# Two attention layers on one core: pairwise maxima for every query block, key, value and row work in one place, and one partial sum kept apart

## The chip, the cores and the metric

The kernel runs on one core of a Trainium2 chip. A core has five engines that run side by side and meet through semaphores: TensorE (PE; its weight loads are shown as PEld), VectorE (DVE), ScalarE (ACT), GpSimd (POOL) and SyncE (SP), which here only issues transfers. The metric is the device time of one execution in microseconds (us). All matrix products are float32.

## The reference

The input x has shape (2, 256, 64, 64). Two layers follow each other; each adds its input to its result.

```python
# layer 0: attention with 8 heads of d = 32 over n = 4096 pixels
qkv = einsum('oc,bchw->bohw', w_qkv, x)              # q, k, v: (b, 8, 32, 4096)
attn = softmax(einsum('bhdi,bhdj->bhij', q, k) / sqrt(32), axis=-1)
out  = einsum('bhij,bhdj->bhdi', attn, v)
x    = einsum('oc,bchw->bohw', w_proj, out) + x
# layer 1: a non-local block; phi and g are pooled 2x2 to 1024 pixels
f = einsum('bnc,bcm->bnm', theta(x[:, :64]), maxpool2(phi(x[:, 64:])))
y = softmax(f, axis=-1) @ maxpool2(g(x))
x = batchnorm(conv1x1(y, W)) + x
```

Layer 0 has 2 x 8 x 4096 x 4096 scores. Its softmax subtracts the row maximum, so all scores are computed twice: once for the maxima, once for the exponentials.

## The kernel before

**Tiling.** The 8 heads go in two quads of four; a quad's four heads of 32 channels fill the 128 partitions. n = 0..3 counts the pairs of batch and quad. A *block* is (n, i): 512 queries (i = 0..7) of the four heads against all 4096 keys. `attend` walks through a block in 32 steps, called *slots* here: slot j takes 128 keys. The loops run over quads, blocks, slots. After the two quads of a batch come `project` (the projection and the residual, which reuses x) and `non_local` (layer 1).

**One slot.** For each of two pairs of heads, `score` (L435) adds a product to the scores in PSUM and ScalarE takes the Exp of both heads at once, 128x1024 (L570). Scores are not recomputed from nothing: PSUM keeps those of the slot before, and the product is with a *difference of keys* (tiles `kd`, `last_kd`, `mid_kd`, `turn_kd`), so that the sum becomes the scores of the next keys. For j = 0 `subtract` (L447) first writes the negative row maximum. `weigh` (L459) multiplies the exponentials of the slot before by v into a scratch tile w, and VectorE adds w to the block's numerator in SBUF (L469; a copy for j = 0, L467). GpSimd adds up the exponentials of heads 0 and 1 (L487); those of heads 2 and 3 are summed by accumulating transfers that GpSimd issues every second slot (L493). `normalize` finishes the block before during the present one: at j = 1 a transfer joins two half sums (L502), at j = 5 GpSimd makes `whole` (L506), at j = 8 TensorE forms the denominators (L514) and ScalarE copies them (L522); SP moves them to DRAM and back so that few elements go to VectorE's reciprocal (L536), and some slots later GpSimd multiplies the numerator by the result (L545).

**Maxima ahead.** The maxima of a block are computed while the block before is in its slots, four slots ahead: the generator `maxes` is advanced twice per slot, each time by two of the four heads. A head's maximum over two chunks of 512 keys can be had in two ways. `plain` (L291): one product per chunk and a VectorE reduction of each (L294). `pair` (L296): max(a, b) = a + relu(b - a); a product with the difference of the two key chunks, a Relu on ScalarE into `over` (L301), a product with the first chunk, and `joint` (L308), a VectorE instruction that adds `over` and reduces both at once; reading its result out is a second short one. `of_head` says which head goes which way: heads 0 and 1 always plain; heads 2 and 3 by pairs, but in a quad's first block (i = 0, n > 0) only for the first half of the keys, as the differences of the second half, `last_kd`, still serve the quad before. After the last step VectorE reduces `part` to `neg` (L376), GpSimd splits that into three bfloat16 terms (`negate`, L141 to L145), and `make_rows` lets TensorE turn them into rows (L150), which ScalarE copies (L158). `first_block` does the very first maxima, all heads by pairs: in each two steps all four heads get their Relu, then all four their joint.

**Makes.** `make` produces a chunk of q, k or v from a chunk of x in the one buffer of the pool `xs` (tag "x"; SP loads it, L88). `during` lists three makes per block, which are done at slots 11, 19 and 27. From k come the differences, all on GpSimd: `differences` (L228), `between` (L237), `rounds` (L240); `renew` places them at the end of a quad's last block and at the start of the next. `late_weights` puts the weights for `project` and `non_local` into the same x buffer after the batch's last make.

**Order.** Each engine runs its instructions in one order. A scheduler makes it: it takes the program's order as priority, and moves an instruction up where its data and buffers allow. `tc.issue_after(ins)` makes what is traced in its block follow ins on ins's engine, and adds no wait. PSUM has four scratch buffers of one bank (`scratch`: products of the maxima, w, makes, rows, denominators, in turn) and two buffers of two banks (`scores`).

## Time and profile before

| what | us |
|---|---|
| median of three runs | 3921.29 (3920.49 to 3923.82) |
| the profiled execution | 3922.07 |
| its span, first to last instruction | 3920.3 |
| batch 0: start, to the first weighing | 0 to 107 |
| a regular block of quads 0 to 2 | 101.9 |
| block (0, 7) | 106.6 |
| a block of quad 3, i = 1 | 99.0 |
| TensorE / VectorE / ScalarE / GpSimd busy | 3884.4 / 2938.6 / 2655.8 / 3050.4 |

Blocks are measured from one block's first weighing to the next one's, from the start times of L459. "Busy" counts a matmul from its start to its modelled end; matmuls overlap, and one that waits for a buffer after its predecessor started can be counted too, so a busy TensorE is not necessarily one that streams. In a line of the timeline the first number is the start in us, the second the duration, the number after x counts merged instructions, and brackets give the idle time before it and what ended it. In a line of groups or windows the busy time stands before the count.

### The profile page before, as it was taken

How to read it: one execution, taken by the hardware profiler on the slowest of the kernel's cores; microseconds unless marked ns; L12 is line 12 of the kernel's file. 1: busy time of each engine (PE TensorE's matmuls, PEld its weight loads, DVE VectorE, ACT ScalarE, POOL GpSimd, SP SyncE). 2: the span in 40 equal slices, each digit the busy share in tenths (PEclk: the TensorE clock that was granted, in tenths of full speed). 3: DMA queues.
4: the chain of work that ended last, by engine and by line, in shares of the span. 5: the costliest groups of instructions: out<-in, count | busy, mean ns of one | idle time of the engine just before them, and what ended most of it. 6: DMA issues, size and time to landing. Idle time of an engine off the chain costs nothing.

```text
span 3920.3 us, 69961 instructions
## 1 busy us (share of the span) xinstructions
PE 3884.4 (99%) x27452; PEld 1374.6 (35%) x27452; DVE 2938.6 (75%) x5483; ACT 2655.8 (68%) x3296; POOL 3050.4 (78%) x1926
## 2 busy tenths in 40 slices
PE   8999999999999999999999999999999999999998
PEld 4333333333333333343333333333433333332333
DVE  5788888888888888874458888888888888884444
ACT  4778777777777777751137777777677788787111
POOL 1788888889888888871448888888899999996043
PEclk9999999999999999999999999999999999999999
DMA  1688888887887888880018888888888888888100
GB/s 57 135 169 169 167 169 169 173 170 166 166 170 166 167 168 168 173 198 6 22 38 167 168 172 170 170 171 174 165 175 168 168 169 169 167 167 184 57 16 27
DMA packets 113931, 569.40 MB, mean 145 GB/s; under 512 B 20296, under 2 KB 22600, under 8 KB 52416
## 3 DMA queue, kind: packets, MB, share of 16 engines
q0 software_dynamic: 68832, 501.25, 63.7%
q1 hardware_dynamic: 44080, 62.88, 4.6%
q8 instruction: 215, 3.52, 0.3%
q14 instruction: 116, 0.95, 0.1%
q10 hardware_dynamic: 688, 0.79, 0.1%
HBM read 54.78 MB, written 8.88 MB: 16 GB/s over the span
## 4 chain that ended last, share of the span: by engine, by line
PE 53%; DVE 2%; DMA 1%; ACT 0%; issue 0%; POOL 0%; DVEq 0%; ACTq 0%; POOLq 0%
PE s L435 14%; PE w L459 13%; PE ps L282 11%; PE y L732 6%; PE g L657 1%; DVE r L746 1%; PE f L700 1%; PE proj L600 1%; PE f L766 1%; PE q L194 1%; PE den L514 1%; PE tp L641 0%; PE tp L637 0%; PE v L182 0%; PE k L194 0%; DMA p<-p 0%
## 5 line engine op out<-in xcount | busy, mean ns | idle before, releaser
L487 POOL TENSOR_TENSOR p<-p,p 128x1024 f32<-128x1024 f32 x945 | 2350.6, 2487 | 375.1 <-ACT p L570 365.2
L570 ACT ACTIVATE p<-s 128x1024 f32<-128x1024 f32 x2048 | 2085.7, 1023 | 594.8 <-PE ps L282 529.1
L282 PE MATMUL ps<-k,q 32*128 32x512 f32 x6232 | 2020.1, 625 | 5.4 <-DVE part L308 3.4
L294 DVE TENSOR_REDUCE part<-ps 128x1 f32<-128x512 f32 x2136 | 1369.8, 686 | 548.0 <-PE ps L282 547.9
L459 PE MATMUL w<-p,v 128*32 128x512 f32 x8192 | 1091.9, 605 | 0.6 <-ACT p L570 0.6
L435 PE MATMUL s<-q,mid_kd 32*128 32x512 f32 x3072 | 766.3, 614 | 0.0
L469 DVE TENSOR_TENSOR y<-y,w 128x512 f32<-128x512 f32 x992 | 678.9, 684 | 59.2 <-PE w L459 58.8
L308 DVE CUSTOM_DVE_ANT_0 ps<-ps,over 128x512 f32<-128x512 f32 x980 | 675.4, 692 | 26.3 <-PE ps L282 23.1
L282 PEld LDWEIGHTS ps<-k,q 32*128 32x128 f32 x6232 | 631.9, 183 | 43.9 <-DVE part L308 10.1
L301 ACT ACTIVATE over<-ps 128x512 f32<-128x512 f32 x916 | 542.4, 592 | 9.2 <-PE ps L282 5.2
L282 PE MATMUL ps<-kd,q 32*128 32x512 f32 x1056 | 520.0, 591 | 0.0
L435 PE MATMUL s<-q,kd 32*128 32x512 f32 x2048 | 512.4, 615 | 0.4 <-ACT p L570 0.3
L435 PE MATMUL s<-q,last_kd 32*128 32x512 f32 x2048 | 510.2, 614 | 1.2 <-ACT p L570 1.2
L459 PEld LDWEIGHTS w<-p,v 128*32 128x32 f32 x8192 | 161.1, 108 | 804.5 <-DVE part L294 774.3
L282 PE MATMUL ps<-last_kd,q 32*128 32x512 f32 x904 | 441.7, 591 | 0.0
L435 PEld LDWEIGHTS s<-q,mid_kd 32*128 32x128 f32 x3072 | 261.8, 183 | 412.7 <-ACT over L301 226.4
L493 POOL DMA_DIRECT2D p<-p x448 | 395.2, 882 | 4.5 <-issue 3.1
L435 PEld LDWEIGHTS s<-q,kd 32*128 32x128 f32 x2048 | 177.7, 183 | 295.7 <-ACT over L301 174.4
L435 PEld LDWEIGHTS s<-q,last_kd 32*128 32x128 f32 x2048 | 177.2, 183 | 276.8 <-ACT over L301 162.7
L732 PE MATMUL y<-p,kv 128*128 128x512 f32 x512 | 240.0, 608 | 6.4 <-DVE r L746 6.4
L781 ACT ACTIVATE p<-f 128x1024 f32<-128x1024 f32 x64 | 65.5, 1023 | 248.5 <-PE f L766 219.2
L728 POOL TENSOR_TENSOR sums<-sums,p 128x512 f32<-128x512 f32 x96 | 121.4, 1264 | 114.3 <-ACT p L781 110.5
(117 smaller groups left out, 2683.2 us busy)
## 6 DMA issues: line engine op xcount, KB each, us to landing
p<-p POOLq DMA_DIRECT2D x478, 1024.0 KB, 7.6
x_q<-in_x_dram SPq DMA_DIRECT2D x30, 512.0 KB
x_k<-in_x_dram SPq DMA_DIRECT2D x24, 512.0 KB
x_res<-in_x_dram SPq DMA_DIRECT2D x16, 512.0 KB
out_dram<-z SPq DMA_DIRECT2D x16, 512.0 KB
r<-flat SPq DMA_DIRECT2D x120, 64.0 KB
x<-in_x_dram SPq DMA_DIRECT2D x8, 512.0 KB
x_v<-in_x_dram SPq DMA_DIRECT2D x6, 512.0 KB
```

Source lines behind the costliest of these rows:

```text
L282: nc.tensor.matmul(ps, q[n, i][bass.ts(h, D), bass.ts(g, P)], keys[bass.ts(h, D), :], start=True, stop=True,)
L294: reduced = nc.vector.tensor_reduce(part[:, g, h, j : j + 1], ps, AX.X, ALU.max)
L301: cut = nc.scalar.activation(over, ps, AF.Relu)
L308: reduced = nc.vector.tensor_tensor_reduce(out=ps, in0=ps, in1=over, scale=1.0, scalar=LEAST, op0=ALU.add, op1=ALU.max, accum_out=part[:, ...
L435: nc.tensor.matmul(s[:, t, :], kj[bass.ts(h, D), :], q[blk.n, blk.i][bass.ts(h, D), :], start=False, stop=True, skip_group_check=j > 0,)
L459: nc.tensor.matmul(w[bass.ts(h, D), :], v[blk.n][:, keys(j), h, :], p[h // 2][:, h % 2, :], start=True, stop=True,)
L469: nc.vector.tensor_add(blk.num, blk.num, w)
L487: added = nc.gpsimd.tensor_add(blk.sums[0], blk.sums[0], p[0])
L493: sent = nc.gpsimd.dma_start(out=blk.sums[n], in_=two, accum_op=ALU.add)
L570: nc.scalar.activation(p[pair], s, AF.Exp, scale=scale)
L728: nc.gpsimd.tensor_add(acc[i][NC], acc[i][NC], p[:, j, :])
L732: nc.tensor.matmul(acc[i][o], wg[:, 2 * t + j, bass.ts(o, P)], p[:, j, :], **edge)
```

## The change

It has four parts.

1. *Maxima by pairs throughout.* `of_head` lets heads 2 and 3 go by pairs in every block. The second-half differences of a new quad are made by GpSimd at slot 8 of the last block of the quad before (`before_all`), into a tile `first_kd` in the x buffer; `pair` reads them there for i = 0. ScalarE copies them to `last_kd` at slots 0 and 2 of the new quad's first block. The first-half differences move from the k make to slots 12 and 14 of block 4. VectorE's reset of `part` goes.
2. *Key, value and rows in one gap.* `during` now gives slots: q at 11, k and v of the same chunk together at 30, where the rows are made too; the last two blocks of a quad differ as shown. The rows get one buffer instead of two.
3. *One sum apart.* In slot j = 26 ScalarE copies w to SBUF (`apart`) in place of VectorE's addition; GpSimd adds it to the numerator at slot 18 of the next block, four steps into what was a wait of 13 steps in `normalize`; the multiplication comes one slot earlier.
4. *First maxima shifted.* In `first_block` heads 2 and 3 run one slot behind heads 0 and 1, so that a slot has the Relus of two heads and the joints of the other two. There is one slot more, and one `advance(maxes)` more.

```diff
-            to = work.tile([P, NB], BF16, tag="rows", name=f"rows_{name}")
+            if layer == 0:
+                to = work.tile([P, NB], BF16, tag="rows", name=f"rows_{name}", bufs=1)
+            else:
+                to = work.tile([P, 2, NB], BF16, tag="over", name=f"rows_{name}")[:, 0, :]
...
-        elif what == "k" and i == NI // 2 - 1:
-            kd[n] = qkv.tile([P, NI // 4, NB], F32, tag="kd", name=f"kd_{n}")
-            for c in range(2):
-                differences(n, c, kd[n][:, c, :])
...
         elif (i, j) == (NI - 1, NJ - 2):
-            differences(n + 1, 2, last_kd[:, 0, :])
             between(n + 1, 2)
-        elif (i, j) == (0, 0):
-            differences(n, 3, last_kd[:, 1, :])
         elif (i, j) == (0, 2):
             rounds(n)
+        if i == 0 and j in (0, 2):
+            nc.scalar.copy(last_kd[:, j // 2, :], first_kd[n][:, j // 2, :])
+    first_kd = {}
     def during(n, i):
         if i < NI - 2:
-            return [("q", n, i + 2), ("k", n + 1, i), ("v", n + 1, i)]
+            return {11: [("q", n, i + 2)], NJ - 2: [("k", n + 1, i), ("v", n + 1, i)]}
         if i == NI - 2:
-            return [("k", n + 1, i), ("k", n + 1, i + 1), ("q", n + 1, 0)]
-        return [("v", n + 1, i - 1), ("v", n + 1, i), ("q", n + 1, 1)]
+            return {
+                11: [("k", n + 1, i), ("v", n + 1, i)],
+                19: [("q", n + 1, 0)],
+                NJ - 2: [("k", n + 1, i + 1), ("v", n + 1, i + 1)],
+            }
+        return {7: [("q", n + 1, 1)]}
+
+    def before_all(n):
+        held.clear()
+        first_kd[n] = xs.tile([P, NI // 4, NB], F32, tag="x", name=f"first_kd_{n}")
+        for c in range(2):
+            differences(n, NI // 4 + c, first_kd[n][:, c, :])
...
-        ps = product(n, i, g, h, (kd[n] if jp < NI // 4 else last_kd)[:, jp % (NI // 4), :])
+        those = kd[n] if jp < NI // 4 else first_kd[n] if i == 0 and n > 0 else last_kd
+        ps = product(n, i, g, h, those[:, jp % (NI // 4), :])
...
     def first_block():
...
+        order = [(jp, g) for jp in range(NI // 2) for g in range(NB // P)]
+        over = {}
+        for slot in range(2 * len(order) + 1):
+            todo = []
+            for two, at in ((0, slot), (2, slot - 1)):
+                if not 0 <= at < 2 * len(order):
+                    continue
+                jp, g = order[at // 2]
+                if two == 0 and at % 2 == 0:
+                    t = double(f"over_{jp}_{g}")
+                    over[at // 2] = t.rearrange("p a b n -> p (a b) n")
+                s = scores(f"ps_{jp}_{g}_{at % 2}") if two else None
+                if at % 2 == 0:
+                    keys = (kd[0] if jp < NI // 4 else last_kd)[:, jp % (NI // 4), :]
+                else:
+                    keys = k[0][:, bass.ts(2 * jp, NB)]
+                for h in (two, two + 1):
+                    ps = product(0, 0, g, h, keys, s[:, h - 2, :] if two else None)
+                    todo.append((ps, over[at // 2][:, h, :], g, h, jp, at % 2))
+            for ps, o, g, h, jp, second in todo:
+                if second:
+                    joint(ps, o, g, h, jp)
+                else:
+                    nc.scalar.activation(o, ps, AF.Relu)
+            yield
...
-        chunks = 0 if h < 2 else NI // 2 if i == 0 and n > 0 else NI
+        chunks = 0 if h < 2 else NI
...
-        if i == 0 and n > 0:
-            nc.vector.memset(part[:, :, 2:, :], LEAST)
...
             if j == 0:
                 nc.vector.tensor_copy(blk.num, w)
+            elif j == NJ - LEAD - 2 and (blk.n, blk.i) != (len(QUAD) - 1, NI - 1):
+                blk.apart = work.tile([P, NB], F32, tag="apart", name=f"w_{blk.name}", bufs=1)
+                nc.scalar.copy(blk.apart, w)
             else:
                 nc.vector.tensor_add(blk.num, blk.num, w)
...
-                for _ in range(13):
+                for _ in range(4):
+                    yield
+            if blk.apart is not None:
+                with tc.issue_after(added.ins):
+                    nc.gpsimd.tensor_add(blk.num, blk.num, blk.apart)
+            if (blk.qd, blk.i) != (QUADS - 1, NI - 1):
+                for _ in range(8):
                     yield
...
+                        if i == NI // 2 and j in (12, 14) and blk.n + 1 < len(QUAD):
...
+                            with tc.issue_after(added.ins):
+                                differences(blk.n + 1, j // 2 - 6, kd[blk.n + 1][:, j // 2 - 6, :])
+                        if (i, j) == (NI - 1, 8) and blk.n + 1 < len(QUAD):
+                            with tc.issue_after(added.ins):
+                                before_all(blk.n + 1)
-                    elif j % 8 == 3 and j > 8 and items:
-                        advance(make(*items.pop(0)), 9)
+                    for item in items.get(j, ()):
+                        if item[1] < len(QUAD):
+                            advance(make(*item), 9)
```

More of the change, by code (lines that the diff above doesn't have):

```diff
@@ L135, in conv_attention, with negate @@
     nc.gpsimd.memset(t, 0.0)
-    def negate(name, neg):
+    def negate(name, neg, layer=0):
         rest = work.tile([P, NB // P, QH], F32, tag="rest", name=f"rest_{name}")
@@ L319, in first_block @@
     def first_block():
-        for jp in range(NI // 2):
-            for g in range(G):
-                over = double(f"over_{jp}_{g}").rearrange("p a b n -> p (a b) n")
-                for what in range(2):
-                    if what == 0:
-                        keys = (kd[0] if jp < NI // 4 else last_kd)[:, jp % (NI // 4), :]
-                    else:
-                        keys = k[0][:, bass.ts(2 * jp, NB)]
-                    s = scores(f"ps_{jp}_{g}_{what}")
-                    ps = [
-                        product(0, 0, g, h, keys, s[:, h - 2, :] if h >= 2 else None)
-                        for h in range(QH)
-                    ]
-                    for h in range(QH):
-                        if what == 0:
-                            nc.scalar.activation(over[:, h, :], ps[h], AF.Relu)
-                        else:
-                            joint(ps[h], over[:, h, :], g, h, jp)
-                    yield
+        order = [(jp, g) for jp in range(NI // 2) for g in range(NB // P)]
[23 more added lines that the diff above has]
+            yield
     G = NB // P
     def of_head(n, i, h):
-        chunks = 0 if h < 2 else NI // 2 if i == 0 and n > 0 else NI
+        chunks = 0 if h < 2 else NI
         pairs = [(g, jp) for jp in range(chunks // 2) for g in range(G)]
@@ L416, in __init__ @@
                 self.last = []
+                self.apart = None
         def keys(j):
@@ L550, in attend @@
                 blk = Block(qd, i)
-                items = [x for x in during(blk.n, i) if x[1] < len(QUAD)]
+                items = during(blk.n, i)
                 both = [None, None]
@@ L583, in attend @@
                                 renew(i, j, blk.n)
-                    elif j % 8 == 3 and j > 8 and items:
-                        advance(make(*items.pop(0)), 9)
+                        if i == NI // 2 and j in (12, 14) and blk.n + 1 < len(QUAD):
+                            if j == 12:
+                                kd[blk.n + 1] = qkv.tile(
+                                    [P, NI // 4, NB], F32, tag="kd", name=f"kd_{blk.n + 1}"
+                                )
+                            with tc.issue_after(added.ins):
[6 more added lines that the diff above has]
+                            advance(make(*item), 9)
         weigh(*waiting)
@@ L710, in maxima1 @@
                 nc.vector.tensor_copy(neg[:, :, 2], neg[:, :, 0])
-                ready.append(negate(f"l1_{b}_{i}", neg))
+                ready.append(negate(f"l1_{b}_{i}", neg, 1))
                 yield
@@ L806, in conv_attention @@
         advance(maxes, G)
+    advance(maxes)
     advance(make("q", 0, 1), 3)
```

## Prediction

> **What bounds the kernel now.** I read the shares first, then the table of windows for whole blocks, then the timelines of TensorE (PE) and VectorE (DVE) at the places that the change touches.[...]
>
> ```profile
> PE 3884.4 (99%) x27452; PEld 1374.6 (35%) x27452; DVE 2938.6 (75%) x5483; ACT 2655.8 (68%) x3296; POOL 3050.4 (78%) x1926
> ```
>
> PE is busy all the way, but pipelined matmuls count as busy while they wait for a buffer, so the length of stages has to decide. Windows of the start, of block (0,7), of the regular block (1,1) and of block (3,2):
>
> ```profile
> core 0: us, PE busy (x) PEld busy (x) DVE busy (x) ACT busy (x) POOL busy (x), PEclk, DMA share, GB/s
> 15.80:80.90 65.10, 61.66 (x313) 26.81 (x312) 45.09 (x129) 37.72 (x72) 8.57 (x7) 1.00 0.01 4
> 820.20:926.80 106.60, 106.60 (x827) 42.26 (x826) 90.24 (x164) 73.69 (x86) 94.03 (x57) 1.00 0.76 159
> 1028.70:1130.70 102.00, 102.00 (x812) 35.07 (x808) 83.27 (x163) 80.03 (x101) 91.50 (x54) 1.00 0.81 168
> 3053.90:3152.80 98.90, 98.90 (x795) 32.98 (x792) 83.16 (x163) 79.01 (x99) 90.38 (x53) 1.00 0.82 169
> ```
>
> In regular blocks no other engine fills its window: a plain slot lasts 2.96 us (weighing starts at 570.00, and at 603.48 and 606.44 in the same timeline), and PE streams through it: six groups of four row-tiled matmuls at 0.43 us, 2.56, plus 0.4 at the two changes of tiling. So a regular block is shortened only by fewer switches. Block (0,7) does the same matmuls and takes 4.7 us more, with VectorE at 90. The start has both engines waiting. TensorE around a k make, a v make and a row transpose:
>
> ```profile
> 570.00 1.06 PE L459 MATMUL w<-p,v 128*32 128x512 f32 x8
> 571.00 1.98 PE L194 MATMUL k<-x_k,wqk_sb 128*128 128x512 f32 x4
> 572.91 0.70 PE L435 MATMUL s<-q,mid_kd 32*128 32x512 f32 x2
> ...
> 596.58 2.05 PE L182 MATMUL v<-wv_sb,x_k 128*128 128x128 f32 x16
> 598.56 0.70 PE L435 MATMUL s<-q,mid_kd 32*128 32x512 f32 x2
> ...
> 607.44 0.40 PE L150 MATMUL pt<-ident_b,terms 128*128 128x128 bf16 x4
> 607.76 0.70 PE L435 MATMUL s<-q,last_kd 32*128 32x512 f32 x2
> ```
>
> From a make's start to the next scores: k 1.91 us, of which four matmuls stream 4 x 0.43 = 1.71; v 1.98, of which 16 x 0.111 = 1.78. Each lone make pays about 0.20 for the switch; the transpose 0.32 for 0.24.
>
> **What the skill says.** TensorEngine Tiling (Array Packing), Key Properties: changing the tiling mode drains TensorE; the 0.20 above agrees. The same page, PSUM Bottleneck: use both ScalarE and VectorE to empty PSUM, which the new ScalarE copy does. GPSIMD Engine Reference, Key points: GpSimd cannot access PSUM and is about 2x slower elementwise; so the copy is needed, and its 128x512 add takes 1.27 us (L237) beside VectorE's 0.68 (L469), 1.9x. DMA: Bandwidth & Descriptors, Latency and other measured facts, puts the fixed cost of a transfer near 2 us; here an 8 KB write issued at 1052.02 lets its successor go at 1056.45, 4.4 us, and I use that.
>
> **Part a, first maxima.** VectorE around one period (a make and four steps, 8 joints):
>
> ```profile
> 31.25 0.70 DVE L308 CUSTOM_DVE_ANT_0 ps<-ps,over 128x512 f32<-128x512 f32 x1
> ...
> 34.17 0.70 DVE L308 CUSTOM_DVE_ANT_0 ps<-ps,over 128x512 f32<-128x512 f32 x1 [2.17 <-PE ps L282]
> ```
>
> The period is 8.11 us (k makes at 30.13 and 38.24); eight of them make the 65 us. VectorE idles 2.2 us in each, because four Relus must run before the first joint, and all four heads turn from Relu to joint together. Half-shifted heads give ScalarE two Relus and VectorE two joints in every slot. Floors of a period: VectorE 8 joints at the spacings that the same timeline has when nothing is missing (0.62, 0.65, 0.65, 0.91 per four) 5.66; PE 8 groups x 0.43 + 1.92 = 5.36; ScalarE 8 x 0.5 + 0.58 = 4.6. I take 6.2, half a microsecond over the highest floor for hand-overs: 8 x 1.9 = 15.3 saved. Ends: 5.7 (19.3) and 7.3 (6.5). The one extra step at the end runs beside the q make.
>
> **Part b, pairs throughout.** In block (0,7) VectorE reduces one by one for heads 2 and 3 too:
>
> ```profile
> 861.23 2.48 DVE L294 TENSOR_REDUCE part<-ps 128x1 f32<-128x512 f32 x4 [0.33 <-PE ps L282]
> ```
>
> Four reduces at 0.60 and the add 0.68 leave nothing over, so slots stretch to 3.4. With pairs a slot has 2 reduces and a joint, as elsewhere. Block (0,7) gives back 106.6 - 101.9 = 4.7 and (0,6), whose last slots already run it (102.5), 0.6; three quads: 16.0. ScalarE's 16 more Relus of 0.59 per quad fit as in regular blocks. The second-half differences move to j = 8 of block 7 (GpSimd, 2 x 1.4 us, needed at about slot 12); they wait for the q make of slot 7 to free the x buffer, and behind them stand the running sums, whose lag of one to three us the probability buffers take.
>
> **Part c, one gap.** k and v share a gap 24 times: 24 x 0.20; the rows join 21 of them: 21 x 0.08; 6.5 saved, ends 0 and 8. The same matmuls run, so nothing else changes. Each x load is issued on SP when the make before it has freed the buffer, at least 8 slots (24 us) ahead, as now; six fewer are issued.
>
> **Part d, weighted sums apart.** One maxima block ends at slot 27. In quads 0 to 2 a make there hides the surplus; in quad 3 nothing does (block (3,1), VectorE, then PE):
>
> ```profile
> 3033.87 1.89 DVE L294 TENSOR_REDUCE part<-ps 128x1 f32<-128x512 f32 x3 [0.39 <-PE ps L282]
> 3035.67 0.69 DVE L308 CUSTOM_DVE_ANT_0 ps<-ps,over 128x512 f32<-128x512 f32 x1
> ...
> 3036.53 0.29 DVE L376 TENSOR_REDUCE neg<-part 128x16 f32<-128x128 f32 x1
> 3036.73 0.68 DVE L469 TENSOR_TENSOR y<-y,w 128x512 f32<-128x512 f32 x1
> ```
>
> ```profile
> 3037.46 1.12 PE L282 MATMUL ps<-k,q 32*128 32x512 f32 x2
> 3038.51 1.07 PE L459 MATMUL w<-p,v 128*32 128x512 f32 x8
> ```
>
> The product at 3037.46 waits for the buffer of w, which the add frees at 3037.41; weighing to weighing is 3.90, 0.95 too long. This add (j = 26) is the one that becomes a copy. ScalarE has no Relu in that slot and stands idle from 3035.78 to 3036.78; w is complete about then, so a copy of 0.59 (L522's 586 ns) frees the buffer near 3036.4; behind it stands the Exp of 3036.78, which waits for scores until then anyhow. I leave 0.2 for the late reduces. Quad 3: 6 x 0.75 saved; quads 0 to 2, where the make leaves slot 27, pay 24 x 0.2 = 4.8. Net +0.3; the bad end is 24 x 0.95 = +23. GpSimd gets 1.27 us per block at slot 18, covered by its 8.5 idle us of 98.9; uncovered it would be 30 x 1.27 = 38.
>
> **Part e, costs.** The one x buffer holds the new differences until two ScalarE copies in the next quad's first block, which overwrite what block (1,7) reads to its last slot. The late weights use that buffer:
>
> ```profile
> 1729.48 0.39 SPq L103 DMA_DIRECT2D weights<-in_wproj_dram  x1
> ```
>
> They now start 14 us before the first projection (1743.9). Afterwards they can start only near 1743.5, behind slot 31 and a copy. Issue plus 4.4 and some transfer ends near 1749: +5.5, once, ends 3 and 8; the residual loads queue behind them on SP but meet an equally late projection. The six ScalarE copies at quad starts, 0.59 against about 0.3 idle per slot: +1 (0 to 3.5). GpSimd near slots 26 to 31 of block 7 loses the make's relief and has three differences, the product and the casts; the j = 31 transfer, the half sum and the denominators may slip, about +2 over three quads, less 0.7 for the 0.9 that block (3,0) loses there now: +1.3. One buffer for the rows costs nothing: written at slot 30, last read at slot 0.
>
> **Sum.** -15.3 - 16.0 - 6.5 + 0.3 + 5.5 + 1.0 + 1.3 = -29.7. The profiled execution took 3922.07 (span 3920.3), 0.8 above the median: 3892.4, less 0.8, 3891.6.
>
> **Rivals.** (1) The first maxima stay bound by their buffers (period 7.6 or more): for it speaks that the two score buffers and four scratch buffers are unchanged; against, VectorE's 2.2 idle us per period. 3891.6 + 11 = 3903, 3898 to 3912. (2) GpSimd becomes the bound: 90.4 of 98.9 busy now, 91.7 then, and about 98 of 98 in block 7. Against: its lag has two or three slots of probability buffers. Some 4 us in each of three transitions and a little per block: 3907. (3) The other side: the copy apart stands behind the next Exp in ScalarE's queue. That Exp waits for scores, the copy would end near 3038.4 and the product 1.0 later than now: 1.9 in each of 24 blocks, 1.0 in six, 52 in all: 3943. It decides from about 1.5 us a block. (4) The parts cancel: handover at its bad end and only half of parts a and c, near 3921.
>
> **How the numbers follow.** Forecast 0.64 (3874 to 3902), rival 1 0.14, rival 2 0.09, rival 3 0.09, rival 4 0.04. Rivals 1 and 2 are still faster by over 0.2% (7.8 us, about what a measurement here can tell): 0.87 faster, 0.04 same, 0.09 slower. The range 3872 to 3912 leaves out rivals 3 and 4 and a little of each tail.
>
> **What would show it.** a: 8 makes 6.2 apart before 66 us, VectorE's 2.17 waits gone. b: blocks (n,7) near 98 us (one make), all slots 2.96. c: pt, k and v in one run of about 3.95 us. d: slot 27 at 3.1 to 3.2 everywhere. e: TensorE waiting some 5 us for the weights after block (1,7). Wrong if slot 27 is 3.9 or more in quads 0 to 2, or if the makes at the start keep their 8 us.

## The result, and the profile after

The changed kernel takes 3907.98 us (median of six, 3904.02 to 3909.10) against 3920.89 before (median of six), a ratio of 0.9965 (0.9955 to 0.9975): 13 us faster, less than half of the 29.7 that were forecast. Its profiled execution took 3908.37, with a span of 3906.6; against the span before (3920.3) that is -13.7, and all sums below are made on these two spans.

The page's shares after the change:

```profile
PE 3864.0 (99%) x27452; PEld 1366.8 (35%) x27452; DVE 2900.7 (74%) x5449; ACT 2697.5 (69%) x3378; POOL 3091.5 (79%) x1957
```

TensorE runs the same 27452 matmuls. VectorE has 38 us less, ScalarE 42 and GpSimd 41 more: the work moved as the change says. The table of windows for the start (up to the q make), block (0,7), the first block of the next quad (1,0), the regular block (1,1) and block (3,2):

```profile
core 0: us, PE busy (x) PEld busy (x) DVE busy (x) ACT busy (x) POOL busy (x), PEclk, DMA share, GB/s
15.70:74.50 58.80, 58.25 (x312) 26.34 (x310) 43.45 (x123) 37.73 (x72) 8.56 (x7) 1.00 0.02 6
817.60:916.30 98.70, 98.70 (x791) 32.67 (x788) 82.82 (x162) 80.65 (x102) 94.42 (x57) 1.00 0.76 154
916.30:1020.40 104.10, 103.50 (x812) 35.89 (x808) 82.89 (x162) 80.48 (x102) 95.93 (x58) 1.00 0.84 179
1020.40:1122.20 101.80, 101.80 (x812) 35.41 (x808) 82.71 (x162) 80.75 (x102) 91.63 (x54) 1.00 0.81 169
3044.10:3142.30 98.20, 98.20 (x796) 32.75 (x794) 82.66 (x162) 79.62 (x100) 91.70 (x54) 1.00 0.82 170
```

Block (0,7) takes 98.7, near the 98 that were forecast, and VectorE is back at 83. Block (3,2) lost 0.8 us, where 0.75 were forecast. But (1,0), 101.9 before, now takes 104.1 with the same matmuls, GpSimd at 95.9 and the highest DMA share. From first weighing to first weighing:

| stretch | before | after | difference |
|---|---|---|---|
| start, to the first weighing | 107.3 | 102.9 | -4.5 |
| blocks 0 to 5 of quads 0 to 2, without (1,0) | 17 x 101.8 | 17 x 101.6 | -3.1 |
| blocks 6 and 7, each of quads 0 and 2 | 102.5 + 106.6 | 105.4 + 98.7 | 2 x -5.0 |
| blocks (1,6) and (1,7), without the wait for weights | | | -4.8 |
| (1,0) | 101.9 | 104.1 | +2.2 |
| (3,0) | 99.8 | 102.6 | +2.8 |
| blocks (3,1) to (3,5) | 5 x 98.95 | 5 x 98.1 | -4.1 |
| wait for the weights beyond the 1.0 us of before, then projection and layer 1 of batch 0 | 291.7 | 4.9 + 295.2 | +8.4 |
| (3,7), projection and layer 1 of batch 1 | 376.9 | 376.2 | -0.7 |

The blocks are nearly where they were forecast. The start, the change of batch (batch 0 to batch 1, between quads 1 and 2) and the first blocks of quads 1 and 3 are not. The -4.5 of the start holds +0.7 from ahead of the first period: the k make of chunk 2 begins at 14.75 here and at 14.01 before, but at 13.48 in the kernel with part 4 alone. From that make to the q make the stretch fell from 64.9 to 59.7, by 5.2. TensorE and VectorE around one make at the start:

```profile
28.57 1.98 PE L197 MATMUL k<-x,wqk_sb 128*128 128x512 f32 x4
30.49 0.70 PE L293 MATMUL ps<-kd,q 32*128 32x512 f32 x2
...
35.92 1.98 PE L197 MATMUL k<-x,wqk_sb 128*128 128x512 f32 x4
```

```profile
29.65 0.73 DVE L320 CUSTOM_DVE_ANT_0 ps<-ps,over 128x512 f32<-128x512 f32 x1
30.30 0.14 DVE L320 DVE_READ_ACCUMULATOR2_ANT part<- 128x1 f32 x1
31.85 0.70 DVE L320 CUSTOM_DVE_ANT_0 ps<-ps,over 128x512 f32<-128x512 f32 x1 [1.40 <-ACT k L211]
32.46 0.14 DVE L320 DVE_READ_ACCUMULATOR2_ANT part<- 128x1 f32 x1
32.75 0.70 DVE L320 CUSTOM_DVE_ANT_0 ps<-ps,over 128x512 f32<-128x512 f32 x1
```

The makes are 7.35 us apart, 8.11 before. VectorE runs eight joints without a hole and then waits 1.40 us (2.17 before): TensorE starts its make at 28.57, VectorE has used up its stock of products by 30.44, and the next products only begin at 30.49. The trace names ScalarE's copy of k as what ended the wait, but that copy starts at 30.60, after TensorE had gone on, and was done 0.7 us before the joint; it is merely the last semaphore to come.

The change of batch, TensorE before and after the projection's start:

```profile
1728.97 1.06 PE L476 MATMUL w<-p,v 128*32 128x512 f32 x8 [1.14 <-ACT p L598]
1734.85 16.30 PE L639 MATMUL proj<-y,weights 128*128 128x512 f32 x32 [4.81 <-DMA weights<-in_wproj_dram]
```

The wait is there, 4.81 us long, near the forecast 5.5. What was not forecast stands in the windows around it:

```profile
1726.00:1732.00 6.00, 2.89 (x24) 0.32 (x16) 3.28 (x6) 2.92 (x4) 5.92 (x5) 1.00 0.82 153
1732.00:1736.00 4.00, 1.15 (x2) 0.67 (x3) 0.00 (x0) 0.00 (x0) 4.00 (x4) 0.59 0.94 271
1736.00:1740.00 4.00, 4.00 (x7) 1.70 (x6) 0.00 (x0) 0.00 (x0) 1.55 (x2) 0.56 1.08 245
1740.00:1744.00 4.00, 4.00 (x10) 1.73 (x10) 1.22 (x1) 0.00 (x0) 0.00 (x0) 1.00 0.99 307
```

From 1732 to 1740 the granted clock (third number from the right) is 0.59 and 0.56, and the first five matmuls of the projection start 0.85 to 0.99 us apart instead of 0.43.

The start of (1,0): GpSimd before the change, where the block begins at 926.76, then GpSimd and ScalarE after it, where it begins at 916.31:

```profile
924.86 0.85 POOL L493 DMA_DIRECT2D p<-p  x1
...
932.50 0.87 POOL L502 DMA_DIRECT2D p<-p  x1 [0.85 <-DMA p<-p]
```

```profile
909.57 0.84 POOL L515 DMA_DIRECT2D p<-p  x1
...
915.22 1.27 POOL L236 TENSOR_TENSOR mid_kd<-k 128x512 f32<-128x512 f32 x1
916.42 0.85 POOL L515 DMA_DIRECT2D p<-p  x1
...
924.76 0.87 POOL L524 DMA_DIRECT2D p<-p  x1 [2.78 <-DMA p<-p]
```

```profile
931.69 1.02 ACT L598 ACTIVATE p<-s 128x1024 f32<-128x1024 f32 x1 [1.90 <-DMA p<-p]
939.28 1.02 ACT L598 ACTIVATE p<-s 128x1024 f32<-128x1024 f32 x1 [2.38 <-POOL whole L528]
```

The accumulating transfer of slot 31 (L515) goes out at 916.42, 0.1 after the end of block (0,7), where it went out 1.9 ahead of that end before; the transfer that joins the half sums (L524, called the half sum below) must wait for its landing; and two Exps wait for the probability buffers that these transfers hold.

### The profile page after: what moved, and what is told of

It reads as the page before. It is cut to its first block, busy times and chain, and to the rows that moved or that the text cites. A ratio compares the mean times of both kernels' runs of the same rounds, so it can differ in the third digit from the quotient of the medians.

```text
span 3906.6 us, 69965 instructions
## 1 busy us (share of the span) xinstructions
PE 3864.0 (99%) x27452; PEld 1366.8 (35%) x27452; DVE 2900.7 (74%) x5449; ACT 2697.5 (69%) x3378; POOL 3091.5 (79%) x1957
## 4 chain that ended last, share of the span: by engine, by line
PE 96%; DVE 2%; DMA 1%; POOL 1%; issue 0%; ACT 0%; DVEq 0%; POOLq 0%; ACTq 0%; SPq 0%
PE s L452 28%; PE w L476 26%; PE ps L293 23%; PE y L771 6%; PE q L197 2%; PE k L197 2%; PE v L185 2%; PE proj L639 1%; PE g L696 1%; DVE r L785 1%; PE f L739 1%; PE f L805 1%; PE den L536 1%; DMA p<-p 1%; PE tp L680 0%; PE tp L676 0%
## 5 line engine op out<-in xcount | busy, mean ns | idle before, releaser
L305 DVE TENSOR_REDUCE part<-ps 128x1 f32<-128x512 f32 x2046 | 1315.7, 686 | 566.8 <-PE ps L293 563.1
L320 DVE CUSTOM_DVE_ANT_0 ps<-ps,over 128x512 f32<-128x512 f32 x1025 | 706.2, 691 | 24.9 <-PE ps L293 10.5
L491 DVE TENSOR_TENSOR y<-y,w 128x512 f32<-128x512 f32 x961 | 659.1, 686 | 51.9 <-PE w L476 49.3
L313 ACT ACTIVATE over<-ps 128x512 f32<-128x512 f32 x961 | 569.3, 592 | 10.7 <-PE ps L293 7.9
L452 PEld LDWEIGHTS s<-q,mid_kd 32*128 32x128 f32 x3072 | 270.4, 183 | 443.5 <-ACT over L313 253.9
L515 POOL DMA_DIRECT2D p<-p x448 | 395.3, 882 | 27.3 <-ACT p L598 27.1
```

Of the source, the lines that this page charges most:

```text
L305: reduced = nc.vector.tensor_reduce(part[:, g, h, j : j + 1], ps, AX.X, ALU.max)
L313: cut = nc.scalar.activation(over, ps, AF.Relu)
L320: reduced = nc.vector.tensor_tensor_reduce(out=ps, in0=ps, in1=over, scale=1.0, scalar=LEAST, op0=ALU.add, op1=ALU.max, accum_out=part[:, ...
L452: nc.tensor.matmul(s[:, t, :], kj[bass.ts(h, D), :], q[blk.n, blk.i][bass.ts(h, D), :], start=False, stop=True, skip_group_check=j > 0,)
L491: nc.vector.tensor_add(blk.num, blk.num, w)
L515: sent = nc.gpsimd.dma_start(out=blk.sums[n], in_=two, accum_op=ALU.add)
```

## Experiments

Each ratio is to the kernel before, measured beside it; the changed kernel's own is 0.9965. An interval reaches about 0.1%, or 2 to 6 us, to each side, so the times alone do not settle differences of 3 or 4 us between two of the changed kernels; there the stretches in the traces carry the argument. Where nothing is said, the kernel computes everything.

### The start: is it the makes?

**Part 4 alone**, the new `first_block` in the kernel before:

```diff
 (kernel before)
-        for jp in range(NI // 2):
+        order = [(jp, g) for jp in range(NI // 2) for g in range(NB // P)]
 ...
+    advance(maxes)
     advance(make("q", 0, 1), 3)
```

> The kernel before with the shifted first maxima alone. Theory (ring of two slots): makes at the start 7.35 us apart instead of 8.11, one longer last period, so the first weighing near 103 us instead of 107.3 and about 3916.5 us. If the step of the prediction had held (6.2 us a period, 15 us) it would be 3906. All other parts are those of before, so nothing else may move.

Measured: 3915.85, ratio 0.9987 (0.9981 to 0.9994). The makes are 7.34 apart, the last stretch from make to q make 9.09, as in the changed kernel; all blocks stay as before. So part 4 is worth 5 us, where the 6.2 us periods would have made it 15, and what is missing at the start is missing in part 4 itself.

**The makes in two halves**, one step apart:

```diff
-        advance(make(what, 0, i), 3)
-        advance(maxes, G)
+        made = make(what, 0, i)
+        advance(made)
+        advance(maxes, 1)
+        advance(made, 2)
+        advance(maxes, G - 1)
```

> The changed kernel with each make among the first maxima cut in two: the half for the first 128 channels before the first step, the other half before the second. Same matmuls. Theory (VectorE starves because one make holds TensorE for 1.92 us and the buffers let it be only one to two slots ahead): the 1.40 us wait per period shrinks below 0.7, periods of 6.4 to 6.7, 3901 to 3903. Rival (the order on ScalarE, where the copy of k stands ahead of the next Relus, or the joints' own spacing sets the period): 7.3 as now, 3908.

Measured: 3905.00, ratio 0.9957 (0.9944 to 0.9969), not clearly apart from the changed kernel's; the period is 7.05, not 6.4 to 6.7. VectorE now waits twice:

```profile
30.45 0.70 DVE L320 CUSTOM_DVE_ANT_0 ps<-ps,over 128x512 f32<-128x512 f32 x1 [0.72 <-issue]
32.53 0.70 DVE L320 CUSTOM_DVE_ANT_0 ps<-ps,over 128x512 f32<-128x512 f32 x1 [0.42 <-PE ps L293]
```

0.72 + 0.42 is little less than 1.40. Either the length of a make is not the point, or something else comes in when a make lies open across a step: its buffer stays taken in the ring of four. The next kernel keeps the make in one piece and shortens it: it leaves out half of the channels in six k makes.

**Half a make**, in one piece:

```diff
-        for c in range(NC):
+        few_c = 1 if what == "k" and n == 0 and i >= 2 else NC
+        for c in range(few_c):
```

> The changed kernel in which the six k makes of chunks 2 to 7 among the first maxima multiply only the first half of the channels (two of the four TensorE stretches, 0.96 us instead of 1.92, are left out, so the first quad's keys are not those of the reference). The place of the make's buffer in the ring of four stays as it is. Theory 1, that the period of 7.35 us is set by how long one make keeps TensorE from VectorE's next products: VectorE's wait of 1.40 us in each period falls by about 0.96, the k periods fall to 6.4 us. Theory 2, that it is the ring, in which the make takes a place until ScalarE has copied it: the wait stays, periods 7.0 to 7.35, as halving the makes in two pieces gave (7.05).

Measured: 3906.66 in one execution; the k makes are 6.66 apart. TensorE's make and VectorE's wait:

```profile
32.41 1.12 PE L198 MATMUL k<-x,wqk_sb 128*128 128x512 f32 x2
39.07 1.12 PE L198 MATMUL k<-x,wqk_sb 128*128 128x512 f32 x2
```

```profile
34.99 0.70 DVE L321 CUSTOM_DVE_ANT_0 ps<-ps,over 128x512 f32<-128x512 f32 x1 [0.72 <-issue]
```

0.86 us less of make gives 0.68 less of waiting. So the wait follows the make's length, to four fifths. The shorter make also gives its buffer back earlier; but in the changed kernel TensorE goes on at 30.49, before the copy of k that frees this buffer has begun, so it is not that buffer that it waits for there. VectorE's stock of products hides a part of every make; a second half that follows a step later finds the stock not yet rebuilt, or its buffer missing (0.42 of waiting more), which is why two halves save only 0.3. Which of the two it is, no run tells apart.

### The pairs, and the weights that they delay

**Part 1 undone** in all quads, the rest kept:

```diff
-        chunks = 0 if h < 2 else NI
+        chunks = 0 if h < 2 else NI // 2 if i == 0 and n in (1, 2, 3) else NI
 ... (no before_all and no copies to last_kd; its differences at (NI - 1, NJ - 2) and (0, 0) as before)
```

> The changed kernel without its first part: in a quad's first block heads 2 and 3 go by single chunks for the second half of the keys again, and the second-half differences are made late, so the x buffer is never held. Theory (the pairs gain 5.0 us at each of three quads and lose 13 at the quads' starts and at the change of batch): about 3910, within 2 of the changed kernel. Rival (the loss lies elsewhere and the pairs are worth their 16 less some 7): 3917.

Measured: 3907.09, ratio 0.9962 (0.9949 to 0.9974): the same as with the pairs. Blocks (0,7) and (2,7) take 101.9 instead of 98.7, and (1,7) 3.0 more up to its last weighing, so the pairs are worth 9.4 us in three quads. In return the projection starts 0.99 us after the last weighing instead of 5.88, and projection and layer 1 take 291.4 instead of 295.2: 8.6 us at the change of batch. (3,0) takes 100.1 instead of 102.6, so 2.5 us of its stall go with the pairs. Gain and costs nearly cancel. (1,0) still takes 104.4: its stall does not come from the pairs.

**Undone for quad 2 alone**, so that the x buffer is free when batch 0 ends:

```diff
-        chunks = 0 if h < 2 else NI
+        chunks = 0 if h < 2 else NI // 2 if i == 0 and n in (2,) else NI
```

> The changed kernel with the first part undone for quad 2 alone, the one whose differences hold the x buffer across the change of batch. Theory (the late weights and the slow clock behind them cost 7 to 8 us there, the pairs bring 5): 3905, the projection of batch 0 starting within 2 us of the last weighing, its matmuls 0.43 us apart from the first. Rival (the weights cost no more than what the pairs bring, the loss is in the layer after): 3908 to 3913.

Measured: 3901.16, ratio 0.9947 (0.9934 to 0.9961), some 7 us better than the changed kernel, more than the 3 expected; the trace shows 8.5 gained at the change of batch and 2.9 lost in (1,7). TensorE's projection here:

```profile
1732.14 14.00 PE L645 MATMUL proj<-y,weights 128*128 128x512 f32 x32
```

Without a wait before it the same 32 matmuls take 14.00 instead of 16.30. The weights thus come with 4.8 of waiting and 2.3 of slow clock, and the clock's share was not in the sum. That a full clock alone would give the 2.3 back is not shown. In the kernel with the differences on VectorE (below) the weights hold TensorE up for only 0.51 us and the matmuls keep their 0.43, but then TensorE stops in the middle:

```profile
1732.15 7.11 PE L641 MATMUL proj<-y,weights 128*128 128x512 f32 x16 [0.51 <-DMA weights<-in_wproj_dram]
1740.96 2.46 DVE L648 TENSOR_TENSOR y<-proj,x_res 128x1024 f32<-128x1024 f32 x2 [8.54 <-DMA x_res<-in_x_dram]
1742.24 7.13 PE L641 MATMUL proj<-y,weights 128*128 128x512 f32 x16 [2.99 <-DVE y L648]
```

VectorE's residual additions wait for their loads of x, which SP issues behind the weights. Late weights thus make these loads late too, and projection and layer 1 take 294.7 there.

### The blocks: sums apart, makes together

**Part 3 undone**: VectorE adds all weighted sums again.

```diff
-            elif j == NJ - LEAD - 2 and (blk.n, blk.i) != (len(QUAD) - 1, NI - 1):
+            elif False:
```

> The changed kernel with part 3 undone: VectorE adds the weighted sum of j = 26 like all others, nothing is kept apart. Theory 1, the copy apart removes a surplus of 0.8 to 0.95 us in slot 27 of every block, since no make stands there any more: regular blocks grow from 101.7 to 102.5, blocks of quad 3 from 98.1 to 98.9, about 28 blocks, +23 us, 3931. Theory 2, the surplus is real only in quad 3 or is taken up by the slots after it: +5 us or less, 3908 to 3913.

Measured: 3928.60, ratio 1.0022 (1.0013 to 1.0031), +21 us against the changed kernel. TensorE at slot 27 of block (3,1) without the copy, and then in the changed kernel:

```profile
3046.51 1.12 PE L293 MATMUL ps<-k,q 32*128 32x512 f32 x2
3047.56 1.06 PE L476 MATMUL w<-p,v 128*32 128x512 f32 x8
```

```profile
3028.12 0.59 PE L293 MATMUL ps<-k,q 32*128 32x512 f32 x1
3028.13 0.77 PE L452 MATMUL s<-q,mid_kd 32*128 32x512 f32 x2
3028.83 1.06 PE L476 MATMUL w<-p,v 128*32 128x512 f32 x8
```

Without it the last product stands alone behind all others, and slot 27, which weighs the exponentials of j = 26, takes 3.90 from weighing to weighing; with it the products run together and the slot takes 3.10. In regular blocks it is the same 0.8 (101.7 to 102.5), since no make stands in slot 27 any more. Without part 3 the kernel is slower than before the change, so part 2 does not pay alone; and rival 3 (the copy stands behind the Exp) is refuted: the copy runs at 3026.86, a microsecond ahead of the Exp.

**Part 2 undone in the blocks i < 6**: k at slot 19 and v at slot 27.

```diff
-            return {11: [("q", n, i + 2)], NJ - 2: [("k", n + 1, i), ("v", n + 1, i)]}
+            return {11: [("q", n, i + 2)], 19: [("k", n + 1, i)], 27: [("v", n + 1, i)]}
```

> The changed kernel with k at slot 19 and v at slot 27 of the blocks i < 6 again, instead of both at slot 30; the rest, the sum apart too, stays. Theory 1, each lone make pays about 0.20 us for the change of tiling and the lone row transposes 0.08: 18 blocks grow by 0.28 to 102.0, +5 us, 3913. Theory 2, joining them gained little, and the 0.2 us between the regular blocks of before and after came from the sum apart: blocks stay at 101.7 to 101.8, 3908 to 3910.

Measured: 3911.93, ratio 0.9975 (0.9967 to 0.9984), +3 to +4 us, which the times alone do not settle; the trace does: blocks take 101.9 instead of 101.7, between the two theories. In the changed kernel transposes, k and v follow each other in TensorE:

```profile
1110.27 0.40 PE L150 MATMUL pt<-ident_b,terms 128*128 128x128 bf16 x4
1110.50 1.94 PE L197 MATMUL k<-x_k,wqk_sb 128*128 128x512 f32 x4
1112.28 1.95 PE L185 MATMUL v<-wv_sb,x_k 128*128 128x128 f32 x16
1114.15 0.70 PE L452 MATMUL s<-q,last_kd 32*128 32x512 f32 x2
```

The gap is 3.88 where three lone ones took 0.32 + 1.91 + 1.98 = 4.21. Of these 0.33 us only 0.17 reach the block: in the changed kernel slot 27 is 0.15 longer than a plain one, and with the lone v make in it, it takes 4.94, a plain slot's 2.96 and the make's 1.98.

### The first blocks of quads 1 and 3

**GpSimd's three differences to VectorE** at the end of block (n,7):

```diff
-        nc.gpsimd.tensor_sub(mid_kd[:, c, :], two[:, NB:], two[:, :NB])
+        eng = nc.gpsimd if n == 0 else nc.vector
+        with tc.issue_after(reduced.ins) if n else ExitStack():
+            eng.tensor_sub(mid_kd[:, c, :], two[:, NB:], two[:, :NB])
```

> The changed kernel with the three differences at slots 26, 28 and 30 of each quad's last block on VectorE (0.7 us each) instead of GpSimd (1.27 us each). Theory 1, GpSimd ends block (n,7) too late, so that its last accumulating transfer and the half sum of the next block's start come late: (1,0) falls from 104.1 to about 101.9 us and (3,0) from 102.6 to about 99, in all 4 to 6 us, 3903. Theory 2, the transfers at (3,0) are slow because the load of x falls on them, and at (1,0) something else is late: no change there, 3908; VectorE then pays some 0.3 us in each of three blocks.

Measured: 3909.76, ratio 0.9969 (0.9956 to 0.9981): no gain in the median. The profiled execution was the fastest of five, 3903.68; the others took 3909.3 to 3910.2, and where their 6 us went no trace shows. In the trace both stalls are gone, (1,0) at 101.7 and (3,0) at 98.1. Blocks (n,7) pay for it, 102.0 and 101.8 instead of 98.7: three slots of 4.2 to 4.6 us, as the difference takes VectorE 1.64, more than twice the 0.7 that was reckoned (the last section shows why):

```profile
L238 DVE TENSOR_TENSOR mid_kd<-k x9: 1480/1644/1791, 894.0 to 2834.0; 128x512 f32<-128x512 f32 x9
```

With the three differences off GpSimd the transfer of slot 31 goes out 5.6 us ahead of the block's end, and no stall follows. So GpSimd's load there is a cause. The next kernels lighten it without VectorE.

**Two differences behind the half sum**, at slot 2 of the next block:

```diff
-        elif (i, j) == (NI - 1, NJ - 4):
-            between(n + 1, 1)
 ... (nor between(n + 1, 2) at NJ - 2)
         elif (i, j) == (0, 2):
+            between(n, 1)
+            between(n, 2)
+        elif (i, j) == (0, 4):
             rounds(n)
```

> The changed kernel in which two of the three key differences that GpSimd makes at slots 28 and 30 of a quad's last block are made at slot 2 of the next quad's first block, behind the half sum's transfer, and the one of slot 2 goes to slot 4. GpSimd does the same work in all, VectorE nothing new. Theory, GpSimd's lag of about 2 us at the end of block (n,7) makes the stalls at the quads' starts: 2 x 1.27 us taken from before that end remove most of it, (1,0) from 104.1 to about 102 and (3,0) from 102.6 to 98.5 to 100, blocks (n,7) stay at 98.7: about -5 us, 3903. Rival, the lag comes from slots before 28, or the differences are now late for the scores of slots 4 and 6: no gain, 3908 or more.

Measured: 3914.71, ratio 0.9984 (0.9978 to 0.9991), worse. GpSimd stands before the half sum's transfer, and the differences behind it are late in TensorE:

```profile
927.00 1.22 PE L453 MATMUL s<-q,mid_kd 32*128 32x512 f32 x2 [4.82 <-POOL mid_kd L236]
```

The same put together with quad 2 plain and halved makes:

> Put together what the runs pointed to: the changed kernel with quad 2 without pairs in the second half of its keys (the weights get their buffer early again), the makes among the first maxima in two halves a step apart, and the two differences at the next quad's start. From 3901 with quad 2 alone: -2.5 for the halves, -4 for the quads' starts if the lag is their cause: 3895. If the lag is not their cause: 3898 to 3899.

Measured: 3909.61, ratio 0.9969 (0.9957 to 0.9980), for the same reason; (1,0) takes 108.6, (3,0) 106.2.

**The two differences at slot 0**, ahead of the half sum:

```diff
 ... (neither at NJ - 4 nor at NJ - 2 any more)
+        elif (i, j) == (0, 0):
+            between(n, 1)
+            between(n, 2)
         elif (i, j) == (0, 2):
             rounds(n)
```

> The changed kernel in which two of the three key differences of slots 28 and 30 of a quad's last block are made at slot 0 of the next block, ahead of the half sum's transfer, where GpSimd now stands idle for 2.8 us; the third and the one of slot 2 stay. In the run with both behind that transfer they were late themselves (TensorE waited 4.82 us for them). Theory, the accumulating transfer of slot 31 is issued too late behind these differences: it goes out 2.5 us earlier, at about 1.9 us ahead of the block's end as in the kernel before; (1,0) falls to about 102, (3,0) to 98.5 to 100, blocks (n,7) stay at 98.7: -5 us, 3903. Rival, the differences at slot 0 are late for the scores of slots 4 and 6 again, or the transfer lands late whenever it is issued: 3908 or more.

Measured: 3904.30, ratio 0.9957 (0.9944 to 0.9969), 3 to 4 us less than the changed kernel, of which the trace shows 1.9 in the two blocks: (1,0) is 103.0 instead of 104.1, (3,0) 101.8 instead of 102.6, so less than half of the stalls went. GpSimd's transfers, (1,0) beginning at 915.4:

```profile
913.07 0.86 POOL L516 DMA_DIRECT2D p<-p  x1
...
922.73 0.87 POOL L525 DMA_DIRECT2D p<-p  x1 [1.66 <-DMA p<-p]
```

The transfer goes out 2.3 us ahead of the end of block (0,7), earlier than in the kernel before, and still the half sum follows only 9.7 us later (7.6 before). Beside it runs the load of x, issued at 909.82; the kernel before issues it 18 us ahead of that end.

**The load of x held back** to SP's transfers of the denominators, as well:

```diff
-            held[b, i] = load_x(b, i, xs.tile([P, NC, NB], F32, tag="x", name=name))
+            with tc.issue_after(bounced.ins) if what == "q" and i == 2 and n % 2 else ExitStack():
+                held[b, i] = load_x(b, i, xs.tile([P, NC, NB], F32, tag="x", name=name))
 ...
+                bounced = nc.sync.dma_start(out=few, in_=flat[0]...)
 ...
-            return {11: [("q", n, i + 2)], ...
+            return {19 if i == 0 and n % 2 else 11: [("q", n, i + 2)], ...
```

> The run with two differences at slot 0, and besides the load of x for the third q make of quads 1 and 3 held back until SP's two transfers of the denominators in the quad's first block (about slot 9), the make at slot 19 instead of 11. The same transfers, but none of x beside the accumulating transfer of slot 31. Across the runs so far the stall at a quad's start has been the issue of the half sum after the block's start, less 6.0 us. Theory, the transfer lands 1.5 to 3 us late because the load of x runs beside it: it lands some 7.6 us after its issue at -2.4, the half sum goes out at +5.3, no stall is left at (1,0) and at most 1 us at (3,0), where two weight loads still fall on it: 101.8 and 98.1 to 99, -4 us, 3900. Rival, the landing is slow whatever runs beside it: 103.0 and 101.8 stay, 3904.

Measured: 3900.08, ratio 0.9948 (0.9935 to 0.9960); (1,0) is 101.7 and (3,0) 98.2, no stall is left. GpSimd's transfers again, (1,0) beginning at 914.7:

```profile
912.35 0.86 POOL L518 DMA_DIRECT2D p<-p  x1
920.04 1.14 POOL L527 DMA_DIRECT2D p<-p  x1
```

7.7 us from issue to the half sum, 2 less than with the load beside it. Most kernels lie on one line: the stall is the issue of the half sum after the block's start, less 6.0 us.

| kernel, block | transfer of slot 31, from the block's start | half sum | stall (block less the regular one) |
|---|---|---|---|
| before, (1,0) / (3,0) | -1.9 / -1.9 | 5.7 / 6.9 | 0 / 0.9 |
| after | +0.1 / 0.0 | 8.5 / 10.5 | 2.4 / 4.5 |
| pairs undone | +0.6 / +0.6 | 8.7 / 8.0 | 2.7 / 2.0 |
| sums apart undone | -0.6 / -1.2 | 7.6 / 10.0 | 1.6 / 4.0 |
| differences on VectorE | -5.6 / -5.6 | 4.0 / 4.3 | 0 / 0 |
| differences at slot 0 | -2.3 / -2.5 | 7.3 / 8.7 | 1.3 / 3.7 |
| and the load of x held back | -2.3 / -2.5 | 5.4 / 6.1 | 0 / 0.1 |

In the table only 3.7 for 8.7 stands off, by one microsecond. Outside it are the two kernels with the differences behind the half sum, where TensorE waits for the differences themselves (stalls of 6.8 to 8.9 for half sums at 7.3 to 8.7). The table shows both causes at once: how late GpSimd issues the transfer, and how long the half sum then follows. Leaving out the kernel with the differences on VectorE, whose half sum hardly waits for the transfer, it follows after 7.4 to 9.5 us without the load of x beside it and after 7.9 to 11.5 with it. The ranges overlap; the pair of kernels that differ in the load alone shows its part, 9.7 against 7.7 at (1,0) and 11.2 against 8.6 at (3,0).

### Put together

The best pieces (quad 2 plain, makes in halves, two differences at slot 0), then with the load of x held back too:

> The same move of two differences to slot 0, with quad 2 without pairs in the second half of its keys and the makes among the first maxima in halves a step apart. 3901 for quad 2 alone, -2.5 for the halves, -5 for the quads' starts: 3894. If the move does not help: 3899 or more.

> The version put together before (two differences at slot 0, quad 2 without pairs in the second half, makes among the first maxima in halves), with the load of x held back as well: 3899 less 4 to 5, 3894 to 3895; without an effect of the load 3899.

Measured: 3898.88, ratio 0.9939 (0.9926 to 0.9953), and 3893.87, ratio 0.9930 (0.9917 to 0.9944). The first missed its 3894: the two differences at slot 0 brought 1.1 us at (1,0) and 0.5 at (3,0), not 5. The second met its forecast. In it (1,0) has no stall, but (3,0) still takes 99.1, with the half sum 9.5 us behind the transfer and no load of x beside it; the cause of that is open. The second is 14 us faster than the changed kernel and 27 faster than the kernel before.

## Where the prediction was right and where it failed

On the spans the forecast was -29.7, the outcome -13.7. Its sums, with what they came to:

| step | forecast | measured |
|---|---|---|
| a, first maxima | -15.3 | -4.5 |
| b, c and d, the blocks | -22.2 | -22.9 |
| e, weights | +5.5 | +8.4 |
| e, quad starts (copies 1.0, GpSimd 1.3) | +2.3 | +6.0 |
| end of the kernel | 0 | -0.7 |

((3,0) is split here: its 0.8 from part 3 and the 0.2 of (1,0) are with the blocks, the stalls with the quad starts.)

**The step that failed is the period of part a**, with 10.8 of the 16 us that are missing. The prediction put VectorE's wait of 2.17 down to the four Relus ahead of the first joint and took it to vanish with the shift. It then took VectorE's floor of 5.66 and half a microsecond "for hand-overs" as the period, and gave the make no wait of its own, since TensorE's own sum, 5.36, was lower. The profile before spoke against this: all heads turn from Relu to joint twice in a period, but VectorE waits only once, each time right behind a make (2.17 before the joints at 26.06, 34.17, 42.28, 50.39 and 58.50). The shift took 0.77 of the wait; the rest belongs to the make, which is not spread over the period but comes in one piece. From its start 1.92 us pass until TensorE's next product begins and 1.36 more until VectorE's next joint, while VectorE's stock lasts 1.87: 1.92 + 1.36 - 1.87 = 1.41, the wait. The period measured 7.35 = 5.95 for eight joints at their spacing + 1.40, and the wait shrank to 0.72 with half a make. A further 1.7 was not in the sum at the end, where the extra step stands before the q make (9.09 against the period of 7.35) and the prediction said that it "runs beside" it. Rival 1 named the right place; that its 3903 (with a period of 7.6) is near the measured time is luck of the other terms. Its reason, the buffers, was only touched: no kernel with a deeper ring was run.

**Parts b to d: the sum right, the shares not.** Blocks (n,7) reached 98.7, the slots in which VectorE had been behind 2.96, and each pair of blocks 6 and 7 gave 5.0. Part b claimed 5.3 of this for the pairs, but they own only 3.2: without them the same two blocks still gain 1.8. Of this 1.8, about 1.1 come from slot 27, which with a make in it took 5.57 us in blocks 6 and 7 (4.94 in the others) and without one takes 3.11 and 2.96; the rest fits the joined makes. In the regular blocks the joined makes gave 0.17 where 0.28 was reckoned, and part 3, worked out from the blocks' -0.18 and this 0.17, cost nothing net in quads 0 to 2 where +0.2 a block was put in. That the sum of the three came out within 0.7 is luck. Part 3 itself was sized well: 0.8 a block in quad 3 against 0.75, and its loss, 21, against the bad end of 23.

**Part e, the weights:** the wait itself was right, 4.9 longer than before against 5.5. The term failed by what it left out. The Trainium skill says what an idle TensorE does next (TensorE: Matmul & The Clock Gate, What's actually happening): after an idle window of about 3.4 us the array's clock falls to half, until it has been busy about as long. The trace agrees on the fall: 4.81 us idle, then five matmuls 0.85 to 0.99 us apart, 2.3 us lost. The slow stretch lasted longer than the page has it, about 5 us here and 3.4 to 6.1 over the seven kernels that idled 4.8 us or more. The prediction also let the residual loads queue behind the weights at no price, because they "meet an equally late projection"; in the kernel with the differences on VectorE they held TensorE up for 2.99. The remaining 1.2 us in projection and layer 1 are no more than kernels without a wait for the weights differ by there (291.4 to 293.0).

**Part e, quad starts:** the price for GpSimd, 2 less 0.7, took the lag as something that the buffers absorb. It saw that a make's relief goes, but not that one transfer at the block's end has a date: the half sum behind it must be on its way 6.0 us into the next block. And that each x load is issued "at least 8 slots (24 us) ahead, as now" was true of when the data are needed, not of what the load meets on its way: the change moved it from 18 to 5.6 us ahead of the block's end, close to that very transfer. Rival 2 had the place (the transitions, about 4 us each, of which two of its three were slow) and, by chance of its other terms, the time.

## What to carry to other kernels

The highest of the engines' sums over a period is reached only if the work comes in small pieces: a long piece on one engine is hidden only as far as the stock of the engine behind it lasts, and the rest is waited for in full. So lay a long piece against that stock, joint by joint, and look in the profile at what each wait stands behind before giving it a cause. Price a wait of several microseconds on TensorE with the slow clock behind it, and a transfer that is moved with what it will run beside, not only with when its data are needed. Parts that each gain can share one buffer, and then the last holder (here the weights) pays; undoing one use at the worst place gave back more than the use was worth.

## What was not expected of the hardware

The slow clock followed every wait for the weights of 3.4 us or more: with 4.8 to 6.0 us of idling the projection's first three to seven matmuls start 0.83 to 0.99 us apart; with 3.45 us (two differences behind the half sum) the first still runs at full rate and the next four start 0.78 to 0.85 apart. The eight kernels whose projection waits less than a microsecond for its weights show 0.43 from the second matmul on, and so does the one that stopped for 2.99 us in the middle, when it goes on. The edge thus lies between 2.99 and 3.45 us in these runs.

A difference of two SBUF tiles of 128x512 took VectorE 1.64 us (1.48 to 1.79, nine of them), the addition of a PSUM tile to one in SBUF 0.69. The Trainium skill (SBUF — State Buffer, Terms) has VectorE and GpSimd share a pair of ports that one of them holds for a whole instruction while the other waits. The traces agree. All nine differences start while GpSimd is inside an instruction and end 0.55 to 0.56 us after it: the one that starts at 908.76 ends at 910.40, GpSimd's addition beside it at 909.85. The changed kernel's last block has the other case too: VectorE adds two SBUF tiles of 128x1024 fifteen times (L507). The eight additions with GpSimd at rest take 1.22 to 1.23; the five that start inside a GpSimd instruction end 1.08 to 1.09 after it, and take up to 1.88:

```profile
3540.87 2.36 POOL L509 TENSOR_TENSOR p<-p,p 128x1024 f32<-128x1024 f32 x1
3542.63 1.69 DVE L507 TENSOR_TENSOR p<-p,p 128x1024 f32<-128x1024 f32 x1
...
3549.24 1.22 DVE L507 TENSOR_TENSOR p<-p,p 128x1024 f32<-128x1024 f32 x1
```

Twice the width took less time with GpSimd at rest than the difference did beside it; from 1.22 for 1024 columns one estimates 0.6 to 0.7 for the difference alone, as was reckoned. What was left out is the wait for GpSimd's instruction.

An accumulating transfer of 1 MB took 7.4 to 9.5 us from issue until the next one that needs it went out, and up to 11.5 with half a megabyte of x beside it. In eight such stretches (two each of before, after, and the differences at slot 0 without and with the load of x held back) the core's DMA engines were on average 68 to 94% busy, and the slowest were not the busiest: 10.5 us at 77% at (3,0) after the change, 8.6 us at 94% with the load held back.
